# Layer 0's sign search in halves around the projection, and layer 1's nine weight buffers in two pools

## The chip, the cores and the metric

One NeuronCore of a Trainium2 chip runs the kernel. The metric is the device time of one launch in microseconds, median of several runs. The engines are PE (TensorE, matmuls), DVE (VectorE), ACT (ScalarE), POOL (GpSimd) and SP (SyncE, which here only issues DMAs). Each engine works through its own list of instructions, and semaphores hold an instruction until what it reads or overwrites is ready.

## What is computed

The input is `x`, 2708 rows of 256 floats, and `adj`, a 2708 × 2708 matrix with about one per cent of positive entries. Four graph layers follow one another, each with a residual and a layer norm around it:

```
x = LN(x + adj @ (x * w0))                          # layer 0
h = (x @ w1) as 4 heads of 64
e = leaky_relu(src[n] + dst[m], 0.2) where adj > 0  # layer 1, masked attention
x = LN(x + LN(softmax(e) @ h) * gamma + beta)
x = LN(x + sign_gru_gat(x, adj > 0, adj < 0))       # layer 2
x = LN(x + [x, (adj @ (x @ nw.T)) / deg] @ lin.T)   # layer 3
```

Layer 2 needs the signs of `adj`, and layer 3 the row sums `deg`. The kernel looks for negative entries while layer 0 streams the matrix, and gets `deg` from a column of ones that stands beside `x` in layer 0's matmul.

## The kernel before

The nodes are cut into 22 tiles of 128 rows (the last has 20). A padded transposed copy of `adj` lies in DRAM as 22 strips: strip t is [128 partitions, 22, 128], 1408 KB in one transfer, and holds everything that layer 0 needs for the 128 output rows of tile t. `load_strip` (L202 to L205) issues that transfer on SP into one of two buffers. A load waits until every reader of the strip two before it has finished.

*The strip loop of layer 0* (L623 to L631, strips 5 to 20; strips 0 to 4 go before it with another order). Strip t is used by

- PE: `strip_matmul` (L211 to L216), 22 steps c0 to c21 that accumulate a 128 × 257 result; each step is two matmul instructions on L213,
- DVE: `layer0_mask` (L453), one instruction of 1.63 us that writes the 0/1 mask of the whole strip as fp8 for layer 1, and the diagonal in `layer0_own` (L462),
- ACT: the sign search of `layer0_own` (L467 to L472): `BELOW` = 6 pieces of the strip, Relu of the negated entries with a running sum, each followed by a read of the accumulator.

When strip t's matmul ends, `layer0_scale` (L477, L478) takes the result out of PSUM and `layer0_rest` (L480 to L486) adds the residual and normalises on DVE, with one power on POOL (L175). Then comes the *projection* of that tile for layer 1, `layer1_projection` (L417 to L445), which runs through all engines in turn: two transposes `tr` on PE, the copy `xt` on ACT (L191), four matmuls `pm` on PE (L423), three exponentials on ACT (`rise` L426, `h` L427, `fall` L429), a product `h` on DVE (L430), a transpose `pf` on PE (L438), the copy `turned` on ACT (L440) and a small DMA to DRAM on POOL (L441, `fall_d`). After tiles 3 and 7 the same function issues the broadcast loads `fall_b` (L415) on POOL, which bring a group's `fall` values to all partitions.

The order on each engine comes from a list scheduler at build time, which takes ready instructions by priority; `tc.issue_after(ins)` adds an edge on the same engine: everything issued within it comes after `ins`. On PE the projection of tile t−2 is spread over strip t: `tr` ahead of c0, `pm` after c1, `pf` after c2. On ACT the six searches of strip t stand ahead of `xt` to `turned` of tile t−2, so PE's last matmul is the last reader of a strip.

*The last strip* (L632 to L650) has 20 rows. Its 22 products are 32 columns wide and fill the PE array in parts (L638, 44 instructions); `parts` on ACT (L648) and `pq` on PE (L495) add the four parts up. The projections of tiles 19, 20 and 21 are spread around its end.

*Layer 1* (L781 to L858) works in pairs of node groups and, for each, in two passes q (two heads each). In a pass it goes over the 22 source tiles c in blocks of two. For each c and head, DVE writes a weight tile `p` (L830 to L834: max of `fall_b` and `rise`, times mask; 1.22 us at full width), in a pool of nine buffers. PE then multiplies: `heads` (L807, `acc` L810) and `totals` (L815, `den` L819), in alternate order from block to block. `step` (L789 to L798) advances what is left of layer 0, the list `rest` (L653), between two parts.

Of the kernel before, what the change touches and what calls it, by code (L numbers as in the profile page):

```python
# [19 lines left out]
P = 128  # L20
# [7 lines left out]
def kernel(  # L28
# [38 lines left out]
    BELOW = 6  # L67

# [114 lines left out]
    copies = []  # L183
# [27 lines left out]
    def strip_matmul(acc, s, n, rhs, between={}):  # L211
        for c in range(NT):
            at = nc.tensor.matmul(acc, s[:, c, :n], rhs(c), start=(c == 0), stop=(c == NT - 1))  # L213
            if c in between:
                with tc.issue_after(at.ins):
                    between[c]()  # L216

# [180 lines left out]
    if True:  # L398
# [12 lines left out]
        if True:  # L411
# [5 lines left out]
            def layer1_projection(pool, t):  # L417
# [12 lines left out]
                nc.vector.tensor_tensor(  # L430
# [4 lines left out]
                )  # L435
# [4 lines left out]
                nc.scalar.copy(turned[:, :n], pf[:H, 0, :n])  # L440
# [10 lines left out]
            with pool("l0", 2) as l0:  # L451

                def layer0_mask(t, s, lo=0, hi=NT):  # L453
                    n = sz(t)
                    nc.vector.tensor_scalar(
# [3 lines left out]
                def layer0_own(t, s):  # L459
                    n = sz(t)  # L460
                    dtmp = st.rearrange("p t i k -> p (t i k)")
                    nc.vector.scalar_tensor_tensor(  # L462
                        dtmp[:n, :n], s[:n, t, :n], 1.0, ident[:n, :n], ALU.mult, ALU.mult,
                        accum_out=diag[:n, t : t + 1],
                    )
                    for i in range(BELOW):
# [151 lines left out]
                falls = [fallp.tile([P, 2, 2 * W], F32, tag="fall_b", name="fall_b") for _ in range(H // 2)]  # L618
                nc.sync.dma_start(gamma_b, bcast(gamma, F))
                nc.sync.dma_start(beta_b, bcast(beta, F))  # L620
                layer0_scale(ahead, last)
                finish(layer0_rest(l0, ahead))
                for t in range(ahead + 2, NT - 1):  # L623
# [3 lines left out]
                    layer0_mask(t, s)  # L627
                    layer0_own(t, s)

                    layer0_scale(t - 1, last)  # L630
                    finish(layer0_rest(l0, t - 1))  # L631
# [3 lines left out]
                if sz(t) <= CT:  # L635
                    for c in range(NT):
                        j = c % TILES * CT
                        nc.tensor.matmul(  # L638
                            acc[j : j + CT, :FE], s[:, c, :CT], x0e[c], start=(c < TILES), stop=(c >= NT - TILES)
                        )  # L640
                else:
                    strip_matmul(acc[: sz(t), :FE], s, sz(t), lambda c: x0e[c])
# [10 lines left out]
            rest = [layer0_rest(l1, NT - 2), layer0_rest(l1, NT - 1)]  # L653
            if sz(NT - 1) <= CT:
                rest.insert(1, layer0_last(NT - 1, parts))
            if True:
# [124 lines left out]
                for g in range(0, len(spans), 2):  # L781
# [7 lines left out]
                    def step(c):  # L789
                        for s in list(steps):  # L790
                            if next(s, s) is s:
                                steps.remove(s)
# [10 lines left out]
                    for q in range(H // 2):  # L803
# [3 lines left out]
                        def heads(c, ps, flags):  # L807
                            for s, (p0, ws) in enumerate(cols):
                                for i in (1, 0):
                                    nc.tensor.matmul(  # L810
                                        acc[s][i * HD : (i + 1) * HD, :ws], hs[c][:, 2 * q + i, :HD],
                                        ps[i][:, p0 : p0 + ws], **flags,
                                    )

                        def totals(c, ps, flags):  # L815
                            for s, (p0, ws) in enumerate(halves_at):
                                for i in (1, 0):
                                    j = (2 * (s ^ q) + i) * CT
                                    nc.tensor.matmul(  # L819
                                        den[j : j + CT, :ws], hs[c][:, 2 * q + i, HD + 1 - CT :],  # L820
                                        ps[i][:, p0 : p0 + ws], **flags,
                                    )

# [885 lines left out]
```

## Time and profile before

| | us |
|---|---|
| time, median of 3 runs | 1854.08 (1852.05 to 1854.89) |
| the profiled execution | 1851.74 |
| its span | 1850.0 |
| busy PE, DVE, ACT, POOL | 1821.8, 1273.9, 699.1, 273.0 |
| granted TensorE clock, mean | 0.996 |

Some places in that execution, in microseconds from the start of its span:

| | from | to |
|---|---|---|
| start of `tr` at strips 5, 6, 7, 8 | 62.57, 74.08, 84.98, 97.12 | |
| the same at strips 20, 21 | 227.98, 238.89 | |
| strip 21's small matmuls, with projections between | 239.48 | 244.19 |
| first pass of layer 1's first pair | 247.16 | 308.81 |

The windows view around that change of layers shows the engines' busy time (with the number of instructions), the granted clock, the DMA share and GB/s:

```profile
core 0: us, PE busy (x) PEld busy (x) DVE busy (x) ACT busy (x) POOL busy (x), PEclk, DMA share, GB/s
228.00:239.00 11.00, 11.00 (x53) 9.28 (x52) 3.23 (x11) 5.06 (x17) 1.86 (x3) 1.00 0.36 131
239.00:247.00 8.00, 7.14 (x65) 3.51 (x67) 6.82 (x12) 2.11 (x11) 3.59 (x5) 1.00 0.24 69
```

In the first window, one strip of the steady loop, PE is busy throughout; in the second, around the last strip, it is not. A line of the timeline gives start, duration, engine, line, operation, what is written and read, and in brackets the idle time ahead of it and what ended it. Several instructions of a kind that follow one another stand in one line with their number (x4). PEld are weight loads, which run beside matmuls; SPq is the issue of a DMA by SP.

### The profile page before, as it was taken

How to read it: one execution, taken by the hardware profiler on the slowest of the kernel's cores; microseconds unless marked ns; L12 is line 12 of the kernel's file. 1: busy time of each engine (PE TensorE's matmuls, PEld its weight loads, DVE VectorE, ACT ScalarE, POOL GpSimd, SP SyncE). 2: the span in 40 equal slices, each digit the busy share in tenths (PEclk: the TensorE clock that was granted, in tenths of full speed). 3: DMA queues.
4: the chain of work that ended last, by engine and by line, in shares of the span. 5: the costliest groups of instructions: out<-in, count | busy, mean ns of one | idle time of the engine just before them, and what ended most of it. 6: DMA issues, size and time to landing. Idle time of an engine off the chain costs nothing.

```text
span 1850.0 us, 23081 instructions
## 1 busy us (share of the span) xinstructions
PE 1821.8 (98%) x7512; PEld 1038.5 (56%) x7512; DVE 1273.9 (69%) x2242; ACT 699.1 (38%) x1443; POOL 273.0 (15%) x447
## 2 busy tenths in 40 slices
PE   9999999999999999999999999999999999999997
PEld 7788842233455886887444444444445556654555
DVE  5344479998797655654658887777887768845664
ACT  3444410023144213111555665555665556321011
POOL 1211110011113411000002000111200202111211
PEclk9999999999999999999999999999999999999999
DMA  8343310000103667764556665454554535634764
GB/s 300 134 149 126 137 43 23 24 1 21 33 7 78 146 146 193 172 146 118 168 140 201 183 175 165 120 167 112 164 157 115 139 101 143 170 91 120 204 171 128
DMA packets 435712, 237.34 MB, mean 128 GB/s; under 512 B 184460, under 2 KB 422445, under 8 KB 433149
## 3 DMA queue, kind: packets, MB, share of 16 engines
q1 hardware_dynamic: 423534, 210.76, 41.9%
q0 software_dynamic: 7696, 20.50, 3.5%
q10 hardware_dynamic: 4350, 4.50, 0.7%
q8 instruction: 62, 1.02, 0.2%
q14 instruction: 70, 0.57, 0.1%
HBM read 223.00 MB, written 12.66 MB: 127 GB/s over the span
## 4 chain that ended last, share of the span: by engine, by line
PE 91%; DMA 3%; DVE 2%; ACT 1%; SPq 1%; issue 1%; POOL 0%; POOLq 0%; DVEq 0%; ACTq 0%
PE m L326 44%; PE acc L810 11%; PE acc L213 8%; PE bank L1192 7%; PE den L819 6%; PE gate L1067 4%; PE bank L1168 3%; PE bank L1235 2%; DMA strip<-in_adj_t_dram 2%; PE m L1436 1%; SPq L273 1%; PE pm L423 1%; PE pq L988 1%; ACT below L469 1%; PE pm L768 0%
## 5 line engine op out<-in xcount | busy, mean ns | idle before, releaser
L831 DVE SCALAR_TENSOR_TENSOR p<-fall_b,rise,mask 128x1024 f32<-128x1024 f32 (+1 forms) x264 | 288.0, 1152 | 25.7 <-PE den L819 15.6
L1333 ACT ACTIVATE p<-st,e_neg 128x1024 f32<-128x1024 f32 (+1 forms) x198 | 197.4, 1040 | 193.9 <-PE m L326 189.3
L326 PE MATMUL m<-s,xq 128*128 128x512 f32 (+3 forms) x660 | 230.1, 467 | 0.0
L810 PE MATMUL acc<-p,h 128*64 128x512 f32 (+2 forms) x1056 | 211.3, 550 | 0.0
L313 DVE TENSOR_TENSOR s<-p 128x512 f32<-128x512 f32 (+3 forms) x132 | 81.5, 618 | 151.7 <-PE m L326 113.3
L326 PE MATMUL m<-p,xq 128*128 128x512 f32 (+1 forms) x396 | 182.9, 543 | 0.1
L213 PE MATMUL acc<-turn,strip 128*128 128x257 f32 x792 | 181.8, 379 | 0.0
L1336 ACT ACTIVATE p<-p 128x1024 f32<-128x1024 f32 (+1 forms) x198 | 178.8, 942 | 0.2
L326 PE MATMUL m<-p,x 128*128 128x512 f32 (+1 forms) x396 | 167.6, 542 | 0.3 <-DVE supt L343 0.3
L326 PEld LDWEIGHTS m<-s,xq 128*128 128x128 f32 x660 | 124.5, 190 | 76.1 <-issue 59.7
L1337 DVE TENSOR_TENSOR p<-p,blk 128x1024 f32<-128x1024 f32 (+1 forms) x132 | 143.0, 1103 | 34.0 <-ACT p L1336 25.9
L213 PEld LDWEIGHTS acc<-turn,strip 128*128 128x128 f32 x792 | 147.2, 190 | 20.3
L810 PEld LDWEIGHTS acc<-p,h 128*64 128x64 f32 x1056 | 72.5, 138 | 132.1 <-issue 123.3
L326 PE MATMUL m<-s,x 128*128 128x512 f32 (+3 forms) x330 | 127.0, 467 | 0.0
L326 PEld LDWEIGHTS m<-p,xq 128*128 128x128 f32 x396 | 74.6, 190 | 76.9 <-issue 61.3
L326 PEld LDWEIGHTS m<-p,x 128*128 128x128 f32 x396 | 74.8, 190 | 75.4 <-issue 60.7
L819 PE MATMUL den<-p,h 128*32 128x512 f32 (+2 forms) x1056 | 112.3, 546 | 0.0
L469 ACT ACTIVATE below<-strip 128x384 bf16<-128x384 f32 x132 | 78.4, 594 | 67.9 <-DMA strip<-in_adj_t_dram 64.5
L284 POOL TENSOR_TENSOR blk<-blk,offdiag 128x128 f32<-128x128 f32 (+3 forms) x50 | 30.6, 617 | 372.4 <-DMA blk<-in_adj_t_dram 295.2
L326 PEld LDWEIGHTS m<-s,x 128*128 128x128 f32 x330 | 62.0, 190 | 39.0 <-issue 34.8
L314 DVE TENSOR_TENSOR p<-p 128x512 f32<-128x512 f32 (+3 forms) x132 | 81.6, 618 | 2.4
L316 DVE TENSOR_TENSOR s<-p,s 128x512 f32<-128x512 f32 (+3 forms) x132 | 81.0, 614 | 2.0
(286 smaller groups left out, 2590.8 us busy)
## 6 DMA issues: line engine op xcount, KB each, us to landing
strip<-in_adj_t_dram SPq DMA_DIRECT2D x19, 1408.0 KB, 6.0
blk<-in_adj_t_dram SPq DMA_DIRECT2D x88, 256.0 KB, 3.5
blk<-in_adj_t_dram SPq DMA_DIRECT2D x88, 192.0 KB, 4.1
pa<-in_adj_t_dram SPq DMA_DIRECT2D x110, 128.0 KB, 2.7
turn<-in_adj_t_dram SPq DMA_DIRECT2D x44, 256.0 KB, 3.1
blk<-in_adj_t_dram SPq DMA_DIRECT2D x88, 128.0 KB, 2.6
p<-in_adj_t_dram SPq DMA_DIRECT2D x88, 128.0 KB, 2.9
turn<-in_adj_t_dram SPq DMA_DIRECT2D x44, 192.0 KB, 3.2
```

The source lines that it names most:

```text
L213: at = nc.tensor.matmul(acc, s[:, c, :n], rhs(c), start=(c == 0), stop=(c == NT - 1))
L313: nc.vector.tensor_tensor(s1, a21, a22, ALU.add)
L314: nc.vector.tensor_tensor(a21, a21, a11, ALU.subtract)
L326: nc.tensor.matmul(dst[:, :w], lt, rt, start=start and not (one_bank and i in (3, 4, 6)), stop=stop and not (one_bank and i in (1, 2, 5)))
L469: nc.scalar.activation(below[:, : (hi - lo) * P], s[:, lo:hi].rearrange("p c n -> p (c n)"), AF.Relu, scale=-1.0, accum_out=negative[:, BE ...
L810: nc.tensor.matmul(acc[s][i * HD : (i + 1) * HD, :ws], hs[c][:, 2 * q + i, :HD], ps[i][:, p0 : p0 + ws], **flags,)
L819: nc.tensor.matmul(den[j : j + CT, :ws], hs[c][:, 2 * q + i, HD + 1 - CT :], ps[i][:, p0 : p0 + ws], **flags,)
L831: nc.vector.scalar_tensor_tensor(p[:, :w], fall_b[:, i, :w], rise[:, c, 2 * q + i : 2 * q + i + 1], mask[:, c, at : at + w], ALU.max, ALU. ...
L1192: nc.tensor.matmul(g[:, :w], lt, rt, start=(q == 0), stop=(q == len(terms) - 1))
L1333: nc.scalar.activation(p[:, :, :w], st_k[:, :, :w], AF.Relu, scale=-1.0, bias=e_neg[:, at, k : k + 1])
L1336: nc.scalar.activation(p[:, :, :w], p[:, :, :w], AF.Exp, scale=-1.0)
L1337: nc.vector.tensor_tensor(p[:, :, :w], p[:, :, :w], blk[:, i, :, :w], ALU.mult)
```

## The change

Five edits, all on order and buffers; no arithmetic is added or taken away.

1. `layer0_own` takes a range, so that a strip's six searches can be asked for in two halves (`FREE` = 3). In the strip loop the first three of strip t come as before, and the second three stand within `issue_after(copies[-1])`: `copies` now also collects the `turned` copies, so they come after the last projection asked for, that of tile t−1.
2. Ahead of the loop, scale and rest of tile 3 stand within `issue_after(projected[0])`: after the product `h` of tile 0.
3. The scale of tile t−1 comes before the searches of t. The rest of tile 19 moves out of the loop into layer 1's list `rest`, which now has three tiles and `layer0_last` ahead of tile 21.
4. The nine `p` buffers become nine named tiles, taken in turn: `p0` to `p3` in the pool `fallp` on the right side of memory, which exists since before the strip loop, `p4` to `p8` in `l1`, whose memory is that of layer 0's pool. The writes of `p` stand within `issue_after(masked)`: after the mask of strip 20.
5. In layer 1, `step` and each part (`heads`, `totals`) stand within `issue_after(product)`: after the last matmul of strip 21 for the first, after the part before for each next.

```diff
@@ -65,6 +65,7 @@
     STEP = 96.0
     SPLITS = 3
     BELOW = 6
+    FREE = 3
 
     sizes = [NT // -(-NT // GT) + (i < NT % -(-NT // GT)) for i in range(-(-NT // GT))]
     spans = [(sum(sizes[:i]), sum(sizes[: i + 1])) for i in range(len(sizes))]
@@ -180,7 +181,7 @@
         mean, rs = moments(src, n)
         nc.vector.tensor_scalar(dst[:n], src[:n], mean, rs, ALU.subtract, ALU.mult)
 
-    copies = []
+    copies, projected = [], []
 
     def transposed(ps, pool, src, n, tag):
 
@@ -214,6 +215,7 @@
             if c in between:
                 with tc.issue_after(at.ins):
                     between[c]()
+        return at
 
     def weights(pool, name, w, queue=nc.sync):
         wt = pool.tile([P, w.shape[0] // P, w.shape[1]], F32, name=name)
@@ -427,17 +429,17 @@
                 nc.scalar.activation(hs[t][:n, :, HD], pm[:n, F + H : F + 2 * H], AF.Exp, scale=ALPHA)
                 fall = pool.tile([P, H], F32, tag="fall", name="fall", bufs=4)
                 nc.scalar.activation(fall[:n], pm[:n, :H], AF.Exp, scale=ALPHA - 1.0)
-                nc.vector.tensor_tensor(
+                projected.append(nc.vector.tensor_tensor(
                     hs[t][:n, :, :HD],
                     pm[:n, H : H + F].rearrange("p (h d) -> p h d", d=HD),
                     hs[t][:n, :, HD:].to_broadcast([n, H, HD]),
                     ALU.mult,
-                )
+                ))
                 yield
                 pf = ps_t.tile([P, 4, P], F32, tag="tr", name="pf")
                 nc.tensor.transpose(pf[:H, 0, :n], fall[:n], ident[:n, :n])
                 turned = pool.tile([H, P], F32, tag="turned", name="turned")
-                nc.scalar.copy(turned[:, :n], pf[:H, 0, :n])
+                copies.append(nc.scalar.copy(turned[:, :n], pf[:H, 0, :n]))
                 nc.gpsimd.dma_start(fall_d[:, t * P : t * P + n], turned[:, :n])
 
                 for g in [g for g, (lo, hi) in enumerate(spans[:2]) if hi == t + 1]:
@@ -452,18 +454,19 @@
 
                 def layer0_mask(t, s, lo=0, hi=NT):
                     n = sz(t)
-                    nc.vector.tensor_scalar(
+                    return nc.vector.tensor_scalar(
                         mask[:, lo:hi, t * P : t * P + n], s[:, lo:hi, :n], 0.0, None, ALU.is_gt, saturate=False
                     )
 
-                def layer0_own(t, s):
+                def layer0_own(t, s, lo=0, hi=BELOW):
                     n = sz(t)
-                    dtmp = st.rearrange("p t i k -> p (t i k)")
-                    nc.vector.scalar_tensor_tensor(
-                        dtmp[:n, :n], s[:n, t, :n], 1.0, ident[:n, :n], ALU.mult, ALU.mult,
-                        accum_out=diag[:n, t : t + 1],
-                    )
-                    for i in range(BELOW):
+                    if lo == 0:
+                        dtmp = st.rearrange("p t i k -> p (t i k)")
+                        nc.vector.scalar_tensor_tensor(
+                            dtmp[:n, :n], s[:n, t, :n], 1.0, ident[:n, :n], ALU.mult, ALU.mult,
+                            accum_out=diag[:n, t : t + 1],
+                        )
+                    for i in range(lo, hi):
                         lo, hi = i * NT // BELOW, (i + 1) * NT // BELOW
                         below = l0.tile([P, -(-NT // BELOW) * P], BF16, tag="below", name="below", bufs=1)
                         nc.scalar.activation(
@@ -616,30 +619,34 @@
                 beta_b = keepr.tile([P, F], F32, name="beta_b")
                 fallp = fall_stack.enter_context(pool("fallp", 2, side="right"))
                 falls = [fallp.tile([P, 2, 2 * W], F32, tag="fall_b", name="fall_b") for _ in range(H // 2)]
+                held = [fallp.tile([P, 2 * W], F32, name=f"p{i}", bufs=1) for i in range(4)]
                 nc.sync.dma_start(gamma_b, bcast(gamma, F))
                 nc.sync.dma_start(beta_b, bcast(beta, F))
-                layer0_scale(ahead, last)
-                finish(layer0_rest(l0, ahead))
+                with tc.issue_after(projected[0].ins):
+                    layer0_scale(ahead, last)
+                    finish(layer0_rest(l0, ahead))
                 for t in range(ahead + 2, NT - 1):
                     s = load_strip(l0, t)
                     last, acc = acc, ps_acc.tile([P, 512], F32, tag="acc", name="acc")
                     strip_matmul(acc[: sz(t), :FE], s, sz(t), lambda c: x0e[c])
-                    layer0_mask(t, s)
-                    layer0_own(t, s)
-
+                    masked = layer0_mask(t, s)
                     layer0_scale(t - 1, last)
-                    finish(layer0_rest(l0, t - 1))
+                    layer0_own(t, s, hi=FREE)
+                    if t < NT - 2:
+                        finish(layer0_rest(l0, t - 1))
+                    with tc.issue_after(copies[-1].ins):
+                        layer0_own(t, s, lo=FREE)
                 t = NT - 1
                 s = load_strip(l0, t)
                 last, acc = acc, ps_acc.tile([P, 512], F32, tag="acc", name="acc")
                 if sz(t) <= CT:
                     for c in range(NT):
                         j = c % TILES * CT
-                        nc.tensor.matmul(
+                        product = nc.tensor.matmul(
                             acc[j : j + CT, :FE], s[:, c, :CT], x0e[c], start=(c < TILES), stop=(c >= NT - TILES)
                         )
                 else:
-                    strip_matmul(acc[: sz(t), :FE], s, sz(t), lambda c: x0e[c])
+                    product = strip_matmul(acc[: sz(t), :FE], s, sz(t), lambda c: x0e[c])
                 layer0_scale(t - 1, last)
                 layer0_mask(t, s)
                 layer0_own(t, s)
@@ -650,9 +657,11 @@
                     layer0_scale(t, acc)
 
             l1 = keep_stack.enter_context(pool("l1", 2))
-            rest = [layer0_rest(l1, NT - 2), layer0_rest(l1, NT - 1)]
+            held += [l1.tile([P, 2 * W], F32, name=f"p{i}", bufs=1) for i in range(4, 9)]
+            held = itertools.cycle(held)
+            rest = [layer0_rest(l1, NT - 1 - i) for i in (2, 1, 0)]
             if sz(NT - 1) <= CT:
-                rest.insert(1, layer0_last(NT - 1, parts))
+                rest.insert(2, layer0_last(NT - 1, parts))
             if True:
 
                 def halves_of(pair, tile):
@@ -787,9 +796,10 @@
                     sums, steps, halves = [], [itertools.chain(*rest)] if g == 0 else [], []
 
                     def step(c):
-                        for s in list(steps):
-                            if next(s, s) is s:
-                                steps.remove(s)
+                        with tc.issue_after(product.ins) if g == 0 else nullcontext():
+                            for s in list(steps):
+                                if next(s, s) is s:
+                                    steps.remove(s)
 
                         if q == 0 and c % 5 == 1 and len(halves) < len(ended):
                             halves.append(layer1_end(l1, ended[len(halves)]))
@@ -807,19 +817,21 @@
                         def heads(c, ps, flags):
                             for s, (p0, ws) in enumerate(cols):
                                 for i in (1, 0):
-                                    nc.tensor.matmul(
+                                    at = nc.tensor.matmul(
                                         acc[s][i * HD : (i + 1) * HD, :ws], hs[c][:, 2 * q + i, :HD],
                                         ps[i][:, p0 : p0 + ws], **flags,
                                     )
+                            return at
 
                         def totals(c, ps, flags):
                             for s, (p0, ws) in enumerate(halves_at):
                                 for i in (1, 0):
                                     j = (2 * (s ^ q) + i) * CT
-                                    nc.tensor.matmul(
+                                    at = nc.tensor.matmul(
                                         den[j : j + CT, :ws], hs[c][:, 2 * q + i, HD + 1 - CT :],
                                         ps[i][:, p0 : p0 + ws], **flags,
                                     )
+                            return at
 
                         fall_b = falls.pop(0)
                         for b, c0 in enumerate(range(0, NT, 2)):
@@ -827,16 +839,18 @@
                             for c in range(c0, min(c0 + 2, NT)):
                                 block[c] = []
                                 for i in range(2):
-                                    p = l1.tile([P, 2 * W], F32, tag="p", name="p", bufs=9)
-                                    nc.vector.scalar_tensor_tensor(
-                                        p[:, :w], fall_b[:, i, :w], rise[:, c, 2 * q + i : 2 * q + i + 1],
-                                        mask[:, c, at : at + w], ALU.max, ALU.mult,
-                                    )
+                                    p = next(held)
+                                    with tc.issue_after(masked.ins):
+                                        nc.vector.scalar_tensor_tensor(
+                                            p[:, :w], fall_b[:, i, :w], rise[:, c, 2 * q + i : 2 * q + i + 1],
+                                            mask[:, c, at : at + w], ALU.max, ALU.mult,
+                                        )
                                     block[c].append(p)
 
                             for i, part in enumerate((heads, totals)[:: -1 if b % 2 == 0 else 1]):
                                 for c, ps in block.items():
-                                    part(c, ps, dict(start=(c == 0), stop=(c == NT - 1)))
+                                    with tc.issue_after(product.ins):
+                                        product = part(c, ps, dict(start=(c == 0), stop=(c == NT - 1)))
                                 if c0 + i < NT:
                                     step(c0 + i)
                         if g + 2 < len(spans):
```

## The prediction

> **What bounds the kernel now.** I read the page's shares first, then its chain, PE's waits, the windows around the end of layer 0, and the timeline of the strip loop.
> ```profile
> PE 1821.8 (98%) x7512; PEld 1038.5 (56%) x7512; DVE 1273.9 (69%) x2242; ACT 699.1 (38%) x1443; POOL 273.0 (15%) x447
> PE 91%; DMA 3%; DVE 2%; ACT 1%; SPq 1%; issue 1%; POOL 0%; POOLq 0%; DVEq 0%; ACTq 0%
> ```
> PE is the bound. A change that takes no matmul away can gain only PE's few gaps, and can lose by opening new ones. PE's list of waits holds two that the edit touches:
> ```profile
> PE pm L423 <- ACT xt L191: 1.8, 3, 1.0
> PE pf L438 <- DVE h L430: 1.6, 1, 1.6
> ```
> The second in the timeline: h0 sits on DVE behind tile 3's scale and norm.
> ```profile
> 49.60 0.41 DVE L485 TENSOR_SCALAR x<-x,bn_mv,bn_rs 128x256 f32<-128x256 f32 x1 [0.66 <-POOL bn_rs L175]
> 49.93 0.74 DVE L430 TENSOR_TENSOR h<-pm,h 128x256 f32<-128x256 f32 x2
> ...
> 50.49 0.27 PE L438 MATMUL pf<-ident,fall 128*4 128x128 f32 x1 [1.59 <-DVE h L430]
> ```
> The strip loop, from the same view. A strip has 22 steps c0 to c21 of two matmuls on PE; `turned` is ACT's last copy of a projection.
> ```profile
> 103.75 0.52 ACT L469 ACTIVATE below<-strip 128x384 bf16<-128x384 f32 x1 [3.31 <-DMA strip<-in_adj_t_dram]
> ...
> 105.69 0.19 ACT L469 ACTIVATION_READ_ACCUMULATOR below<-strip 128x1 f32 x1
> ...
> 108.35 0.74 PEld L213 LDWEIGHTS acc<-turn,strip 128*128 128x128 f32 x4
> 108.47 0.33 SPq L204 DMA_DIRECT2D strip<-in_adj_t_dram  x1
> ...
> 111.63 0.57 POOL L441 DMA_DIRECT2D fall_d<-turned  x1 [0.41 <-ACT turned L440]
> 114.33 1.63 DVE L455 TENSOR_SCALAR mask<-strip 128x2816 fp8e4<-128x2816 f32 x1 [2.33 <-DMA strip<-in_adj_t_dram]
> ```
> The load leaves when PE drops the old strip (108.47), lands 5.86 us later (the mask starts), and PE wants it at the next c0, 119.26: five us to spare, no PE gap. The end of layer 0 in the chain:
> ```profile
> 239.48 0.56 PE acc L638 x6
> 240.04 1.09 PE pm L423 x4
> 241.13 0.56 PE acc L638 x4
> 241.69 0.20 PE pf L438
> 241.89 2.30 PE acc L638 x34
> ...
> 244.21 0.38 ACT parts L648
> 244.59 0.38 ACT xt L191
> ...
> 245.01 1.17 PE pm L423 x4
> ...
> 246.83 0.32 PE pq L495
> 247.16 1.07 PE den L819 x6
> ```
> The last strip's 44 small matmuls are cut up by projection 19, and projection 20 with `pq` stands, latency exposed, before layer 1's first `den`.
>
> **What the Trainium skill says.** "Perfetto Trace Analysis", section "Tensor Engine Instruction (MATMUL, LD_WEIGHTS)": the other engines run strictly in order, PE lets only weight loads ahead. The trace agrees: `xt` sat behind six searches at 87.00, `pm` waited 0.96 us for it. "DMA: Bandwidth & Descriptors", section "Queues, rings and completion order": an SDMA engine takes turns between queues packet by packet. The trace is less even. The timeline shows strip 7 issued behind the two `fall_b` loads of the first group:
> ```profile
> 71.62 1.47 POOL L415 DMA_DIRECT2D fall_b<-fall_d  x2 [4.16 <-DMA fall_d<-turned]
> ...
> 74.52 0.33 SPq L204 DMA_DIRECT2D strip<-in_adj_t_dram  x1
> ```
> Its mask started at 82.76, 8.24 us later; for the last twelve strips issue to mask took 5.80 to 6.31, mean 5.94. What stood first went first, so here the measurement decides over the page.
>
> **Part by part** (profiled execution: span 1850.0, 1851.74 in all; the median of runs, 1854.08, is 2.3 above, and the difference carries over).
>
> *h0 first.* The product of tile 0 on DVE gates `pf`, and with it everything behind it on PE. With it ahead of scale(3) and rest(3) the 1.59 wait goes: `fall`, the other thing `pf` waits for, was done by 48.81. Scale(3) and rest(3) come later by one product (0.4), which PE needs only a strip later. What is late next is nothing: PE's list has no other wait there. −1.59.
>
> *Searches in halves.* On ACT, six searches of t used to stand ahead of xt..turned of t−2. Now: xt..turned(t−1), three of t, three of t+1, xt..turned(t). The searches wait for their strip; where it lands late they hold the projection. That happened once: strip 7 landed at 82.76, its six searches ran to 87.00, `xt` behind them, and that period of PE, from `tr` to `tr`, was 12.14 (weight loads at 84.98 and 97.12) against a steady 10.905 (108.02 to 118.93). Now `xt` is ahead of them. −1.23.
>
> The price: a strip has two buffers, and the load of t+2 waits for all readers of t. The last was PE's c21; it becomes ACT's second half, queued behind `turned` one strip later. SP holds only this load there; behind it is PE's next-but-one strip. From the rows: c0 108.35 to the start of `turned` 111.08 is 2.73; next ACT instruction 0.21; three searches 103.75 to 105.88 are 2.13; to SP's issue 0.05: 5.11, where it was 0.12. Plus 5.94 landing: 11.05 between c0's against 10.905, so PE is held 0.145 per strip. Strip 7 by its own rows 0.16, strips 8 to 21 14 × 0.145 = 2.03. Bounds: landing 5.80 gives 0.005 each, 6.31 gives 0.515 (+7.2 in all). I take the mean. +2.19.
>
> *fall_b of the second group* (POOL, 115.31, 4.23 after `turned`) now starts inside strip 10's load. Bounds: 0, or the whole transfer, 3.7 by the 8.24 landing with its issue time. By turns, four 4 KB packets between the strip's last four of eight 11 KB ones: 16/88 of some 4 us, 0.7. I take 0: the strip stands first.
>
> So c0 of strip 21 comes 1.59 + 1.23 − 2.19 = 0.63 earlier.
>
> *Strip 21 to the first den.* The 44 matmuls now run on end: 2.30/34 = 0.0676 each, 2.97, where 239.48 to 247.16 was 7.68. −4.71. p0 to p3 are written behind strip 20's mask, before 236; tile 20's norm ends near 242.4 (3.3 after its scale), p4 to p7 follow at 1.22 each, 243.7 to 247.5; PE wants p5 near 247.2 and p7 near 249. Cover 1.5 us or less; if norm(20) is late, PE waits for p by that much.
>
> *Layer 1's first pass* takes over projections 19 and 20 and `pq`. From the chain's runs (`den` x32 3.57, x8 1.00; `acc` x32 7.02, x16 3.58) a `den` matmul costs 0.1075, an `acc` one 0.215, and 0.14 for each change between them. Before: 176 × 0.3225 = 56.76, 21 runs 2.94, projection 21 1.0: 60.7; measured 247.16 to 308.81, 61.65, so 0.95 unexplained. After: `issue_after(product)` keeps heads and totals in whole blocks, 16 runs, 2.24; three projections at 0.22 + 0.89 + 0.11, 3.66; `pq` 0.43: 63.1. +1.45; if the 0.95 comes again, +2.4. Their results are needed blocks later, so latency is covered.
>
> Sum −0.63 − 4.71 + 1.45 = −3.9: 1850.2, and 1847.8 for a profiled execution. Later layers keep their order; the first load of layer 2 waits on the same last reader. "TensorE: Matmul & The Clock Gate", section "Part 1: The HAM clock gate", says that PE falls to half clock when a window shows it little used. The trace has one such dip, late and away from the edit (granted clock 0.97 in the window 550 to 600 us, so 50 × 0.03 = 1.5 us lost); it may come or go, and widens the range by that much on both sides.
>
> **Rivals.**
> *The loop doesn't bind.* If release or landing is 0.15 shorter than counted (`mask` starts a little after the landing itself), the 2.19 goes: −6.1, 1848.0. For it: the margin is thin. Against: no load was under 5.80.
> *Collision and small leftovers.* `fall_b` holds strip 10 by 3 us or so, or the 0.95 recurs with late p's: −0.9 to +0.5, some 1853.8. For it: strip 7's 8.24. Against: here the strip is first in its queue.
> *Slower: the strip load becomes the loop.* Place: the wait of L204's load for ACT's second half. Every 0.1 us beyond 5.11 + 5.94 is paid 14 times, 1.4 us. The gain of 6.1 is spent at an excess of 0.43 (5.11 + 6.23), and at 0.71 the run is 3.8 us slower; I put this case at 1858.5. For it: single landings of 6.31, and a load that is issued late has no slack to lose one in; against: the twelve steady loads scatter little, and nothing else of size but `fall_b` is on the DMAs then.
> *It doesn't do what it says.* PE's and SP's own orders in the loop are as before, and ACT's is as described; only the list scheduler's whole-block order in layer 1 could fall short, within 0.7 us.
>
> **How the numbers follow.** Forecast 0.60 (−2.5 to −6, 1848 to 1851.6), no binding 0.17, collision 0.09, slower 0.14. 0.2% is 3.7 us, about what a measurement can tell from no change; the forecast lies just beyond it: 0.38 of its 0.60 beyond, 0.22 within. Faster 0.38 + 0.17 = 0.55, same 0.22 + 0.09 = 0.31, slower 0.14. Range: low end from no binding with a kind clock (−7.6), 1846.5; high end through the collision into the slower case's first third, 1855.8.
>
> **What would show it.** Right: no wait at `pf` near 50; `xt` directly behind `tr` in every strip; SP's load some 5.1 us after c0 and `acc` L213 waiting about 0.1 to 0.2 us for DMA in each strip from 8 on; 44 `acc` L638 in one piece; p writes ahead of the last mask. Wrong: PE's waits name the strip's DMA with over 6 us in sum, or DVE p in the first blocks, or strips 8 to 21 keep a period of 10.9 (no binding).

## The result, and the profile after

| | before | changed |
|---|---|---|
| median of 22 runs each, us | 1853.62 | 1850.02 |
| lowest to highest | 1850.01 to 1855.97 | 1845.76 to 1853.87 |
| ratio, 95% interval | | 0.9981 (0.9975 to 0.9987) |
| the profiled execution, its span | 1851.74, 1850.0 | 1851.49, 1849.7 |

The change saves 3.6 us. In a later series of runs the ratio was 0.9986 (0.9979 to 0.9993). The two profiled executions happen to lie closer together than the medians, so the time is followed from place to place in them rather than read from their spans. All lines are now shifted by a few: L189 to L190, L438 to L440, L213 to L214, L638 to L645, L819 to L830, L810 to L820.

The page of the changed kernel, busy time and the chain's shares:

```profile
PE 1822.9 (99%) x7512; PEld 1039.6 (56%) x7512; DVE 1267.4 (69%) x2242; ACT 698.7 (38%) x1443; POOL 297.1 (16%) x447
PE 92%; DMA 3%; DVE 2%; SPq 1%; ACT 1%; issue 1%; POOL 0%; POOLq 0%; DVEq 0%
```

PE stays the bound. The timeline at the place where `pf` of tile 0 had waited 1.59 us for `h`:

```profile
48.67 0.18 ACT L431 ACTIVATE fall<-pm 128x4 f32<-128x4 f32 x1
...
48.91 0.27 PE L440 MATMUL pf<-ident,fall 128*4 128x128 f32 x1
```

`pf` follows `fall` at once, and its line has no bracket any more. The strip loop, in the timeline of the changed kernel:

```profile
108.74 0.26 ACT L442 COPY turned<-pf 4x128 f32<-4x128 f32 x1 [0.36 <-PE pf L440]
...
110.84 0.19 ACT L472 ACTIVATION_READ_ACCUMULATOR below<-strip 128x1 f32 x1
...
111.05 0.33 SPq L205 DMA_DIRECT2D strip<-in_adj_t_dram  x1
111.92 1.51 POOL L417 DMA_DIRECT2D fall_b<-fall_d  x2 [1.47 <-issue]
...
117.11 1.63 DVE L457 TENSOR_SCALAR mask<-strip 128x2816 fp8e4<-128x2816 f32 x1 [6.22 <-DMA strip<-in_adj_t_dram]
117.13 0.73 PEld L214 LDWEIGHTS acc<-turn,strip 128*128 128x128 f32 x4 [0.19 <-DMA strip<-in_adj_t_dram]
```

The load leaves SP at 111.05, right behind the third late search, and has landed when the mask starts at 117.11, 6.06 us later. PE's weight load of c0 starts 0.02 us after it, and is the one that shows the wait (0.19). The kernel before had five us to spare here. The chain of waits around the end of layer 0:

```profile
232.54 6.20 DMA strip<-in_adj_t_dram
...
238.79 2.58 PE acc L645 x42
...
241.59 1.72 PE den L830 x14
243.30 7.02 PE acc L820 x32
250.32 0.37 PE tr L190 x2
250.69 1.85 PE den L830 x16
252.54 1.09 PE pm L425 x4
```

A strip's load is now part of the chain, which it was nowhere in this stretch before. The last strip's matmuls run on end, the first `den` follows without a gap, and projection 19 sits inside layer 1.

A table of two stretches serves for all that follows. *Loop* runs from the second `tr` ahead of the strip loop (weight load at 46.22 before, 46.27 after) to the weight load of strip 21's first small matmul (239.41, 238.79). *End* runs from there to the first `den` of layer 1's second pass (308.81, 305.46).

| | loop | end | sum |
|---|---|---|---|
| before | 193.19 | 69.40 | 262.59 |
| changed | 192.52 | 66.67 | 259.19 |

The sum is 3.40 shorter, near the 3.6 of the medians. Two more profiled executions of the same two kernels, described below, give 263.59 and 259.32, 4.27 apart, so the sum itself moves by almost a microsecond. In this one execution nearly all of it is lost again far away: between 1525 and 1550 us the granted clock was lower than in the profile of before. The windows view, first before, then changed (busy times with counts, then clock, DMA share, GB/s):

```profile
1525.00:1550.00 25.00, 23.51 (x82) 14.48 (x81) 18.95 (x43) 16.18 (x27) 10.30 (x14) 1.00 0.59 153
```
```profile
1525.00:1550.00 25.00, 22.78 (x75) 14.18 (x74) 17.34 (x41) 15.13 (x26) 10.25 (x14) 0.93 0.49 129
```

25 × 0.07 = 1.75 us, an estimate. The other 1.3 us or so are lost in the later layers too, where small waits of PE were longer (in its list of waits, `bank` for `yt` 2.5 us where it was 1.7, `gate` for `xt` 0.8 where there was none); that part wasn't followed further. So the spans differ by 0.3 only.

### The profile page after: what moved, and what is told of

Read it like the earlier page. It is cut to its first block, busy times and chain, and to the rows that moved or that the text cites. A ratio compares the mean times of both kernels' runs of the same rounds, so it can differ in the third digit from the quotient of the medians.

```text
span 1849.7 us, 23045 instructions
## 1 busy us (share of the span) xinstructions
PE 1822.9 (99%) x7512; PEld 1039.6 (56%) x7512; DVE 1267.4 (69%) x2242; ACT 698.7 (38%) x1443; POOL 297.1 (16%) x447
## 4 chain that ended last, share of the span: by engine, by line
PE 92%; DMA 3%; DVE 2%; SPq 1%; ACT 1%; issue 1%; POOL 0%; POOLq 0%; DVEq 0%
PE m L328 43%; PE acc L820 11%; PE acc L214 8%; PE bank L1206 7%; PE den L830 6%; PE gate L1081 4%; PE bank L1182 3%; PE bank L1249 2%; PE acc L519 2%; SPq L275 1%; PE pm L425 1%; PE m L1450 1%; DMA strip<-in_adj_t_dram 1%; PE pq L1002 1%; ACT below L472 1%
## 5 line engine op out<-in xcount | busy, mean ns | idle before, releaser
L820 PE MATMUL acc<-p,h 128*64 128x512 f32 (+2 forms) x1056 | 210.5, 549 | 0.0
L214 PE MATMUL acc<-turn,strip 128*128 128x257 f32 x792 | 182.6, 381 | 0.3 <-DMA strip<-in_adj_t_dram 0.2
L214 PEld LDWEIGHTS acc<-turn,strip 128*128 128x128 f32 x792 | 147.2, 189 | 22.0 <-DMA strip<-in_adj_t_dram 1.4
L820 PEld LDWEIGHTS acc<-p,h 128*64 128x64 f32 x1056 | 72.7, 138 | 129.7 <-issue 122.2
L457 DVE TENSOR_SCALAR mask<-strip 128x2816 fp8e4<-128x2816 f32 (+5 forms) x40 | 39.3, 1012 | 109.2 <-DMA strip<-in_adj_t_dram 109.2
L830 PE MATMUL den<-p,h 128*32 128x512 f32 (+2 forms) x1056 | 110.5, 546 | 0.0
```

Source lines behind the costliest of these rows:

```text
L820: at = nc.tensor.matmul(acc[s][i * HD : (i + 1) * HD, :ws], hs[c][:, 2 * q + i, :HD], ps[i][:, p0 : p0 + ws], **flags,)
L830: at = nc.tensor.matmul(den[j : j + CT, :ws], hs[c][:, 2 * q + i, HD + 1 - CT :], ps[i][:, p0 : p0 + ws], **flags,)
```

## The experiments

Times are given as the ratio to the kernel before on the same chip, with a 95% interval; the stretches are those of the table above, each from one profiled execution. The *period* of a strip is the time from its `tr` to the next strip's.

**Sizes of the halves.** Four kernels change one constant of the changed kernel, `FREE`: how many of the six searches stand ahead of the projection. In the loop PE's order is the changed kernel's with four, five and six ahead.

```diff
-    FREE = 3
+    FREE = 4
```


> The changed kernel with four searches ahead of the projection and two behind it. My theory (each strip is paced by release plus load, 11.05 us): the release comes one search, 0.76 us, earlier, so 4.36 + 5.94 = 10.30 is under PE's own 10.905; the period from tr to tr is 10.905 in every strip from 8 on, strip 21 begins near 236.6 instead of 238.8, and the time is 2.2 us below the changed kernel's, near 1847.8. Rival (the longer period comes from loads that land while PE and ACT read, or from another order, not from the wait): the period stays near 11.06 and the time near 1850.

Ratio 0.9968 (0.9958 to 0.9978), median 1847.01; loop 192.31, end 66.68. The steady period is 10.905 in 12 of 14 strips, so the wait is what had lengthened it. Strip 21 didn't begin 2.2 earlier, though: two single loads took 7.48 and 7.22 us, and their strips' periods were 11.89 and 11.63. A slack of 0.6 us doesn't cover such loads. This execution, at 1849.39, was among the slowest of its 13, 2.4 above their median.

```diff
-    FREE = 3
+    FREE = 6
```


> The changed kernel with all six searches ahead of the projection, as before the change; everything else of the change stays. My theory: the strip is released by PE again, period 10.905, but strip 7 is held by the group loads and its searches hold xt once (12.14): strip 21 begins near 237.8, 1.0 us earlier than in the changed kernel, and the time is near 1849.0. So the halves cost more than they gain. Rival (the halves are the source of the gain): slower than the changed kernel by 1 to 3 us, 1851 to 1853.

Ratio 0.9964 (0.9954 to 0.9974), median 1845.63; loop 191.60, end 66.68. All periods from strip 7 on are 10.905 but its own, 12.38. The halves as put in by the change are a loss of 0.9 us in the profile; in the medians of runs more, and the rival is out. The ratio puts the time 6.6 us under before, where its two stretches give 4.3 to 5.3 under the two profiles of before. The profiled execution took 1847.60, 2.0 above the median; what the faster ones did otherwise isn't shown, and the interval reaches to 4.8.

```diff
-    FREE = 3
+    FREE = 2
```


> The changed kernel with two searches ahead of the projection and four behind. My theory: the release comes one search later, 5.87 us after c0, and 5.87 + 5.94 = 11.81 is the period from strip 8 on; 14 strips at 0.905 over 10.905 are 12.7 instead of 2.4, so the time is some 10.5 us above the changed kernel's, near 1860.5. Rival (the release isn't what paces the loop): 1850 to 1852.

Ratio 1.0014 (1.0004 to 1.0023), median 1854.16; loop 197.49, end 66.67. Slower, so the release does pace the loop, but by half of what was expected: 5.0 us above the changed kernel's loop, not 10.5. The periods mostly alternate, 11.63 and 10.91 to 11.2. On PE `pm` now stands ahead of c0 in every second strip, where the changed kernel has it behind c1 in all. The timeline of one such strip:

```profile
83.39 0.35 PEld L190 LDWEIGHTS tr<-ident,x 128*128 128x128 f32 x2
...
84.44 1.16 PE L425 MATMUL pm<-w_a,xt 128*128 128x264 f32 x4 [0.46 <-ACT xt L192]
```

PE waits for `xt` (the first matmul of `pm` comes 0.84 us after `tr`'s at 83.60), but does `pm` at a time when it would wait for the strip anyway (these strips landed 0.8 to 2.3 us after `tr`; the one shown was there when `pm` began). The release then mostly comes 5.98 us after `tr` instead of 6.12 or more, which helps the next strip. That this order is what halved the loss wasn't tried by itself. The edit changed one constant and with it an order on another engine, which the expectation had left out.

```diff
-    FREE = 3
+    FREE = 5
```


> The changed kernel with five searches ahead of the projection and one behind. My theory: the release comes 1.5 us earlier than in the changed kernel, 3.6 us after c0, and 3.6 + 5.94 = 9.5 leaves PE's 10.905 a slack of 1.4 us, so that even loads of 7.2 to 7.5 us, as single ones took with four ahead, hardly hold PE. xt stands ahead of a late strip's searches as in the change. From the second tr before the loop to strip 21: 190.4 us, where the kernel before took 193.3, the changed kernel 192.5, four ahead 192.4, six ahead 191.7. Time 5.5 us below before, ratio 0.9970. Rival (what counts is only that PE is the last reader, not the slack): as with four ahead, single holds of 0.7 to 1.0 us stay.

Ratio 0.9967 (0.9951 to 0.9982), median 1846.95; loop 190.11, end 66.67. Every period from strip 7 on is 10.905. One of them in the timeline:

```profile
117.01 0.35 PEld L190 LDWEIGHTS tr<-ident,x 128*128 128x128 f32 x2
...
120.97 0.33 SPq L205 DMA_DIRECT2D strip<-in_adj_t_dram  x1
...
127.04 1.63 DVE L457 TENSOR_SCALAR mask<-strip 128x2816 fp8e4<-128x2816 f32 x1 [5.84 <-DMA strip<-in_adj_t_dram]
127.92 0.35 PEld L190 LDWEIGHTS tr<-ident,x 128*128 128x128 f32 x2
```

The load leaves 3.96 us after `tr` and lands about a microsecond ahead of the next `tr`; the slowest (6.48) is covered. This is the expected 190.4 and is 5.8 us under before in the sum, 6.1 by the ratio of runs. Against six ahead the ratio of runs shows no gain (0.9964 there); in the profiles the two differ by strip 7's hold.

**The weight buffers.** All nine buffers back in layer 1's pool; the order edges and the late projections stay:

```diff
-                held = [fallp.tile([P, 2 * W], F32, name=f"p{i}", bufs=1) for i in range(4)]
...
-            held += [l1.tile([P, 2 * W], F32, name=f"p{i}", bufs=1) for i in range(4, 9)]
-            held = itertools.cycle(held)
...
-                                    p = next(held)
+                                    p = l1.tile([P, 2 * W], F32, tag="p", name="p", bufs=9)
```


> The changed kernel with all nine weight buffers in layer 1's own pool, as before the change; order edges, late projections and halves stay. My theory: p0 can't be written before layer 0's pool is free, so DVE starts on p after norm 20, near 242.0; the last strip ends on PE near 241.4 and the first den waits for p1 (244.5), the second tile's for p3 (246.9): the first pass ends 4.5 us later than in the changed kernel, and the time is near 1854.5. Rival (the gain at the end comes from taking the projections out of the last strip alone, and DVE keeps up anyway): within 1 us of the changed kernel, 1850 to 1851.

Ratio 1.0005 (0.9996 to 1.0013), median 1853.22; loop 191.93, end 73.16. The end is 6.5 us longer (4.5 expected), longer even than before the change. Its chain, then PE's first matmuls of layer 1 in the timeline, then PE's clock in the windows view:

```profile
241.22 0.06 DVE x L488
...
242.75 1.34 DVE p L841 x2
244.08 1.05 issue
245.14 1.45 DVE p L841
...
246.63 1.93 PE den L827 x8
248.56 7.85 PE acc L817 x32
```
```profile
244.08 1.94 PE L827 MATMUL den<-p,h 128*32 128x512 f32 x8 [2.88 <-DVE p L841]
```
```profile
243.40:250.20 6.80, 5.51 (x20) 0.94 (x22) 6.80 (x6) 0.00 (x0) 2.89 (x2) 0.50 0.23 64
```

DVE goes from norm 20 to p, and the chain is on it until p3; PE, done with the last strip by then, stands. The two first tiles came close to the expected times. Most of the 2.0 us beyond the expectation is the clock: towards the end of the 2.88 us in which PE stood the granted clock fell to 0.50 for 6.8 us, and eight `den` took 1.93 where eight take 1.00 at full clock in the kernel before, 32 `acc` 7.85 where they take 7.02, 1.8 together. Even without that the end is longer than before the change: taking the projections out of the last strip gains nothing without p tiles written ahead. Early p tiles without the late projections weren't run.

**The parts alone.** First the kernel before with the loop's edits only (h0 first, halves, the scale ahead of the searches); pools, projections of tiles 19 to 21 and layer 1 as before:

```diff
+                with tc.issue_after(projected[0].ins):
+                    layer0_scale(ahead, last)
+                    finish(layer0_rest(l0, ahead))
...
+                    layer0_own(t, s, hi=FREE)
...
+                    with tc.issue_after(copies[-1].ins):
+                        layer0_own(t, s, lo=FREE)
```


> The kernel before with the loop's edits alone (h0 first, halves); weight buffers, projections of the last tiles and layer 1 as before. My theory: from the second tr before the loop to strip 21 192.5 instead of 193.3, the rest as before (69.3 from strip 21's first small matmul to the end of the first pass): 0.7 us below before, less where single slow loads fall: ratio 0.9996 to 1.0003. Rival (the halves are the gain): the whole 3.6 us, 0.998.

Ratio 1.0016 (1.0009 to 1.0022), median 1855.33; loop 193.32, end 73.85. Slower than before, where 0.7 faster was expected. The loop's own part is a wash (+0.1), and the end, which was taken as unchanged, lost 4.45. The timeline, and PE's clock in the windows view:

```profile
249.47 0.35 ACT L192 COPY xt<-tr 128x256 f32<-128x256 f32 x1
...
249.88 2.12 PE L425 MATMUL pm<-w_a,xt 128*128 128x264 f32 x4 [4.53 <-ACT xt L192]
```
```profile
247.60:254.40 6.80, 4.53 (x14) 1.67 (x16) 6.80 (x7) 2.46 (x10) 2.01 (x2) 0.50 0.14 38
```

Strip 20's three late searches and strip 21's six all stand on ACT between `turned` of tile 19 and `xt` of tile 20, and projection 20 is still ahead of layer 1 on PE, which waits 4.5 us. The clock adds to it: it was 0.50 for 6.8 us here, where it was 1.00 in the same window of before, and these four `pm` took 2.12 us where they had taken 1.17. In the full change that projection lies in layer 1, and nobody waits: edits 3 and 4 cover a debt of edit 1.

Then the end's edits only, the changed kernel with `FREE = 6` and without the edge for h0:

```diff
-    FREE = 3
+    FREE = 6
...
-                with tc.issue_after(projected[0].ins):
+                if True:
```


> The changed kernel without the halves and without h0 first: only the end's edits stay (projections of tiles 19 and 20 in layer 1, four weight buffers beside layer 0). My theory: the loop takes 193.3 as before, from strip 21's first small matmul to the end of the first pass 66.7 instead of 69.3: 2.7 us below before, ratio 0.9985. Rival (the end's gain is given back later, at layer 1's end or layer 2's start): 0.9995 to 1.0000.

Ratio 0.9986 (0.9977 to 0.9996), median 1849.35; loop 191.77, end 66.67. As expected, 2.7 us in the end's stretch and 2.6 by the ratio. The loop held a surprise: strip 7 had a period of 10.905 here, with nothing changed for it, as its load took 6.80.

And h0 alone on the kernel before, the first edit of the loop's diff above by itself:

> The kernel before with one edit: the product of tile 0 ahead of scale and rest of tile 3 on DVE. My theory: the third tr before the loop comes 2.64 after the second instead of 4.28, nothing else moves: 1.6 us below before, ratio 0.9991. Rival (the wait is only moved on): 1.0000.

Ratio 0.9997 (0.9988 to 1.0006), median 1851.13; loop 191.74, end 69.40. The third `tr` follows 2.64 after the second where it was 4.28, and the loop is 1.45 shorter (strip 7 was held 0.18 longer). In the time, 1.6 us is within the interval and so is nothing: inconclusive there.

**Strip 7 and the group loads.** All six searches ahead, and the first group's `fall_b` loads behind the DMA of tile 5:

```diff
-                nc.gpsimd.dma_start(fall_d[:, t * P : t * P + n], turned[:, :n])
-                for g in [g for g, (lo, hi) in enumerate(spans[:2]) if hi == t + 1]:
-                        load_fall(dst, g, q, nc.gpsimd)
+                sent = nc.gpsimd.dma_start(fall_d[:, t * P : t * P + n], turned[:, :n])
+                for g in [g for g, (lo, hi) in enumerate(spans[:2]) if max(hi, 6) == t + 1]:
+                        with tc.issue_after(sent.ins):
+                            load_fall(dst, g, q, nc.gpsimd)
```


> All six searches ahead, and the broadcast loads of the first group are issued two tiles later, behind the small DMA of tile 5. My theory: the hold at strip 7 (period 12.38 with six ahead) comes from those loads standing ahead of strip 7 in the DMA engines; two strips later they have over 4 us of lead on the strip load and it goes: strip 7 lands in 6 us, its period is 10.905, and from the second tr before the loop to strip 21 it takes 190.2 to 190.5, as with five ahead; time 5.5 us or more below before, ratio 0.9970 or lower. Rival (strip 7's period is long for another reason, the start of the loop): 12.4 stays, or moves to the strip that is behind the loads now.

Ratio 0.9971 (0.9960 to 0.9981), median 1847.38; loop 191.36, end 66.68. Strip 7's hold went (10.905), as it had in the run with the end's edits alone, where the loads weren't moved; strip 11 got a period of 12.15, behind the second group's loads, which this edit doesn't touch and which had held nobody so far. The timeline there:

```profile
112.56 1.80 POOL L417 DMA_DIRECT2D fall_b<-fall_d  x2 [2.89 <-DMA fall_d<-turned]
116.83 0.33 SPq L205 DMA_DIRECT2D strip<-in_adj_t_dram  x1
...
125.08 1.63 DVE L458 TENSOR_SCALAR mask<-strip 128x2816 fp8e4<-128x2816 f32 x1 [4.71 <-DMA strip<-in_adj_t_dram]
```

Issued 4.27 us behind the group loads, the strip took 8.25 us. In the profile of before the same pair stood 4.07 apart and the strip took 5.87. So a lead of 4 us isn't a cover. The kernel before, profiled once more:

> The kernel before, a second look, for strip 7 alone: with the same issue times its load took 8.24 us before and 8.48 with six ahead, but 6.80 with the end's edits alone. If the group loads always stand in its way, it takes over 8 us again and the period of that strip is 12.1 to 12.4; if it differs from execution to execution, 6 to 8.5 us and 10.9 to 12.4 are open, and the 1.23 us that the prediction took from it is a gain only in some executions.

Loop 194.19, end 69.40. Here strip 7 took 8.51 (period 12.40) and strip 11 8.34 (12.24), both held. Five profiled executions have all six searches ahead and the group loads in their old place (before twice, six ahead, h0 alone, the end alone). Four had strip 7 held and one had strip 11 held: it differs from execution to execution, with the same order and nearly the same distances (2.7 to 3.0 us ahead of strip 7, 3.8 to 4.2 ahead of strip 11). The wait that h0 first removes isn't a constant either: in this execution the third `tr` came 3.67 after the second, not 4.28.

**The changed kernel beside five ahead**, on one chip:

> The changed kernel again, beside five ahead on the same chip. My theory: released 5.0 us after c0, every strip is held by what its load takes over 5.9 us; the 14 periods from strip 7 on add up to 152.7 plus 2 to 4 us, and single loads of over 7 us, if they come, count in full. Time 3.6 us below before, ratio 0.998.

> Five searches ahead, again, beside the changed kernel. My theory: 14 periods of 10.905, strip 21 2.3 us or more earlier than in the changed kernel counted from the second tr before the loop, ratio to before 0.9965 to 0.997, and 2 to 3 us below the changed kernel. Rival (the difference between the two was the chip's or chance): equal to the changed kernel within 1 us.

The changed kernel again: ratio 0.9986 (0.9979 to 0.9993), median 1849.50; loop 192.65, end 66.67. Five ahead: 0.9970 (0.9958 to 0.9981), median 1846.70; loop 190.10, end 66.68. The loop differs by 2.55, the medians by 2.8. Five ahead beats both kernels.

## Why the prediction was right

The forecast was 3.9 us faster; it is 3.6. The places and the waits were right, and the nearness of the sum is in part luck: two of its terms were read from one execution and turn out to differ from execution to execution, and a third came near through two errors that offset each other. Step by step, in the profiled pair:

| step | forecast | measured | where |
|---|---|---|---|
| h0 first | −1.59 | −1.64 | second to third `tr`, 4.28 to 2.64 |
| strip 7 not held | −1.23 | −1.23 | 12.14 to 10.91 |
| load waits for the late half | +2.19 | +2.41, +2.55 | `tr` 7 to strip 21: 155.38, again 155.52, less 152.97 with five ahead |
| group loads in strip 10's load | 0 | 0 | landed in 6.06, again 6.27 |
| last strip and first pass | −3.26 | −2.73 | 69.40 to 66.67 |
| `tr` of tile 19 leaves the loop | not counted | −0.2 | what is left of the 3.40; two `tr` take 0.22 |

*h0.* Right in size and place for this pair. It was shown in the profile with the edit alone; in the time of runs it is too small to be seen alone. In the second profile of before the wait was shorter, and the same step would be −1.03.

*Strip 7.* Right for the pair of profiles, but not a constant. The prediction took the one hold that the profile of before had for a property of that kernel. Its second profile had two, and the kernel with the end's edits alone none, so the term lies between 0 and 2.8. How the hold arises was read rightly: a late strip's six searches stand ahead of `xt` on ACT, and every strip whose load took over 8 us had a period of 12.1 to 12.4. What removes it stays open. With `xt` ahead no projection was held at strip 7 in either profile of the changed kernel, but there the load left at 77.87, after the group loads of 69.99, and took 5.86 and 5.74 us, so that no late strip put `xt` to the test. The prediction had seen the new place of the loads only as a danger; at strip 10 the load now stands ahead of them (111.05 against 111.92).

*The late half.* The mechanism was right: SP's load leaves right behind the late search in every strip, 5.37 us after `tr` where PE wasn't held, where 5.44 had been worked out, and five ahead gives the 10.905 back. The size was 0.2 to 0.4 short, and near by luck. With the true release and the mean load of strips 8 to 21, 5.98, the same sum gives 5.04 + 5.98 − 10.905 = 0.12 per strip and 1.6 in all. It came to 2.4 since loads took 5.6 to 6.6: a slow one holds PE, and a fast one gives nothing back. The recorded mean of 5.94 is that of strips 10 to 21; its upper bound, 6.31, is strip 8's. The prediction judged the split only inside the change. Here it was a loss: giving ACT one late search instead of three keeps `xt` ahead and costs no period. That even one late search is better than none isn't shown by the times (0.9967 and 0.9970 against 0.9964 with none).

*Group loads in strip 10.* Taken at 0, and right within the spread of the loads: the strip landed in 6.06 and, again, 6.27. What stood first went first: in the trace's DMA records the strip's pieces start from 112.00 to 116.19 us, the groups' from 115.94 to 119.63. The prediction put such a measurement over the Trainium skill ("DMA: Bandwidth & Descriptors", "Queues, rings and completion order"), but that section needn't differ: by it an engine drains a whole packet, typically 9 to 17 descriptors, before it switches. The trace has 128 pieces of 11 KB and 16 closing words for a strip, nine for each of 16 engines; if each of the nine is a descriptor, they may be a single packet.

*The end.* The sum of −4.71 and +1.45 was 0.5 too good, and the runs show that it is one figure, 66.67 in every kernel with all of the end's edits, to 0.01. The mis-sized term is the price of the late projections: `tr`, `pm` and `pf` of tiles 19 and 20 took 0.37, 1.09 and 0.20 inside layer 1's blocks where 0.22, 0.89 and 0.11 were counted (the first two are the strip loop's; `pf` takes 0.23 there, and 0.11 only for tile 21 with its 20 rows), and `pq` 0.54 for 0.43; together 0.99, and the first pass was 64.09 (241.37 to 305.46) where 63.1 was forecast. The last strip's 44 matmuls made two fifths of it good, 2.58 to the first `den` for 2.97. On the other side the sum left out that `tr` of tile 19 no longer stands in the loop. The 0.95 us that the prediction's sum couldn't explain before the change didn't come again.

One reason given there stays open. Whole blocks of `den` and `acc` were put down to `issue_after(product)`. No run leaves these edges out by themselves. The run with the loop's edits alone has neither them nor early p tiles, and from its second block on PE also goes through `den` and `acc` in runs of 16 to 32, so blocks can be whole without them. That PE needs the early p tiles is shown by the run with one pool.

The prediction named one dip of the clock in the profile of before. That profile has two more stretches under 1.00, 0.97 from 1600 to 1650 us and 0.94 from 1800 to 1850; the changed kernel has these three too, and the one that it has besides lies between 1525 and 1550.

The slower rival named the right place, the wait of the load, and gave a price of 1.4 us per 0.1. It stayed below its turning point, 6.23, because loads average 5.98, and 6.02 again; the run with two searches ahead went past it. The rival that the loop doesn't bind is out. What the prediction didn't see is the tie between the loop's edits and the end's: alone, the loop's edits make the kernel slower, since nine searches pile up ahead of `xt` of tile 20.

## What to carry to other kernels

A buffer's last reader sets when the next load starts, so an edit that moves a reader on an idle engine must be priced as release plus load against the period of the bound engine, and needs slack for single slow loads besides. When work is put off in every step of a loop, see what it stands ahead of after the last step. Of several edits that belong together try each alone: here two of the three searches put behind the projection were pure cost, and with five ahead and one behind the kernel beats both, the changed one by 2.8 us; with all six ahead it is as fast. And follow a stretch in more than one profiled execution before its waits are priced: two of the waits counted here as gains were shorter, or absent, in others.

## What was not expected of the hardware

A 1408 KB strip issued 2.7 to 4.3 us behind two 512 KB group loads landed in 8.2 to 8.5 us in six cases, and in 5.75 to 6.8 in five others at nearly the same distances; with the strip first by 0.9 us it took 6.06 and 6.27. Without any other large load near, most strips from 8 on took 5.6 to 6.6 us, and single ones 7.1 to 7.5; none took 8. Which it will be isn't settled by any run here.

In the two kernels where PE stood 2.88 and 4.53 us at the end of layer 0, the granted clock was 0.50 for 6.8 us around the end of that wait. In the twelve other profiled executions, where PE stands a microsecond or less there, it was 1.00. So a wait of a few microseconds cost more than itself: the matmuls behind it were slower too.

A wait of PE for a strip shows under PE's weight loads: the list of PE's waits gives 0.2 us for `acc` L214 in the changed kernel and that of the weight loads 1.4, while the periods add up to 2.4. The periods are the better measure.
